# Expert tiles of two units of 128 slots with single units for the odd rest, in a fused deformable-convolution and expert kernel

## The chip, the core and the metric

The kernel runs on one core of a Trainium2 chip. The core has five engines with a queue of instructions each: PE (TensorE, matrix products), DVE (VectorE), ACT (ScalarE), POOL (GpSimd, which here only issues indirect DMAs) and SP (SyncE, which issues plain DMAs). Each engine works through its queue in order and waits on semaphores for the others; 16 DMA engines move the data. The metric is the device time in microseconds (us) of one execution of the whole program. Everything is computed in 32-bit floats.

## The reference

The input x has 4 images of 256 channels and 64 x 64 pixels. One layer is applied: three modulated deformable 3x3 convolutions with a residual, and then, on every pixel as a token of 256 values, a mixture of 8 experts with a residual. Cut to what matters here:

```python
x = x + conv3(ln_c(x))                    # three deformable convolutions with relu
t = to_tokens(x)                          # 4 x 4096 tokens of 256 values
z = ln_t(t)
probs = softmax(z @ gate_w + gate_b)      # 8 experts
top2_vals, top2_idx = top_k(probs, 2)
for e in range(8):                        # W1[e] is 256 x 512, W2[e] is 512 x 256
    y = gelu(z @ W1[e] + b1[e]) @ W2[e] + b2[e]
    out += cw[:, e] * y                   # cw: the top-two probability, else zero
t = t + out
```

The kernel computes each expert only for the tokens that chose it: each token takes two *slots*, one with each of its two experts.

## The kernel before, in words

**Convolutions.** An image is cut into 8 blocks of 512 pixels. A block of a layer takes nine *taps*; a tap makes four indirect gathers on POOL (L511, 128 rows of 4 KB, 0.52 MB each) of the four pixels around each sampling point, mixes them on DVE (L517, L522) and scales them on ACT (L525), turns them on PE (L540) and multiplies them with the tap's weights (L557). There are 4 x 3 x 8 = 96 blocks, 864 taps. Nine buffers hold gathered rows, so POOL can run about two taps ahead.

**Groups of tokens.** The tokens of images 0, 1 and 2 form three groups (0, 1, 2) of 4096 tokens, image 3 two groups (3, 4) of 2048. When the last block of a group is through, its lane `routes` runs `route` (L701): for each of the 128 x M tokens of a group (M is 32 or 16), from the ranks of its experts, the place of its two slots. Experts follow each other in a list of slots, and each expert's part is rounded up to whole tiles of FT = 256 slots, so that a tile has one expert. `NF` (L91) is the number of tiles that is always run, enough for the worst case: 2 x 32 x 128/256 + 7 = 39 in a large group, 23 in a small one, 163 in all. `invert` (L779) makes the list of tokens by slot (`tok`) with matmuls on one-hot matrices, and `wrow` holds for each tile the rows of the weight table that it needs.

**A tile.** `fetch` (L801) gathers the tile's weights on POOL (L811; 2308 floats on each of 128 partitions, 1.18 MB) and its tokens' rows (L823, one gather of 128 rows of 1 KB for each unit of 128 slots). The weight gather moves nothing where the tile before it in the list has the same expert (L764 to L766 set its rows out of bounds). Tiles are run in the order of `order` (L96): one from the first half of the list and one from the second in turn, each half with a weight buffer of its own (`w[step % 2]`). `expert` (L836) runs a tile in three pieces: four transposes of the rows (L851) and a copy to `zT` (L855); W1 as matmuls of 128x256 into `ph` (L867) and gelu (L877); W2 into `py` (L885). The trace counts 16 matmuls a tile at L867 and 16 at L885. The next tile is fetched between the second and the third piece, or ahead of the second while draining. `products` adds the bias on DVE (L903, which reads the weight buffer) and stores the tile to `ys` through SP (L906); it is called at the start of the next tile. When all tiles of a group are through, `combine_fetch` gathers each token's two results (L926), `combine` adds them weighted to the token (L941), and `give` turns and stores them.

**The order of the work.** Instructions are written out in one program order, and three lanes weave the expert work into the taps: after each tap `pump` gives every lane a credit of one tap, and a piece runs when its price is covered. A piece of a tile costs a third of the group's `pace`, in taps: 5, 6, 2, 1.5 and 0 for groups 0 to 4 (L983). At the end of some stages and of the program, `drain` runs pieces without taps, and group 4 is run wholly so. Each engine's queue keeps this order: a wait at one instruction holds all behind it.

## Time and profile before

| | |
|---|---|
| median of 3 runs | 6497.67 us (6488.08 to 6500.29) |
| the profiled execution | 6500.16 us |
| its span, first to last instruction | 6498.1 us |
| PE, DVE, POOL, ACT busy | 6025.0, 4960.6, 4424.2, 3330.6 us |
| moved by DMA | 2228.45 MB |

The span runs from the first to the last instruction of the profiled execution; about 2 us lie around it. In the groups of the profile, a line gives the source line, engine, operation, output and inputs, the shape and the count, then the busy time in us and the mean duration of one in ns, and then the time the engine stood idle just before these instructions with what ended it. In a table by stretch, each row gives the stretch in us from the span's start, its length, the busy time (and number of instructions) of PE, of PE's weight loads, of DVE, ACT and POOL, PE's granted clock, the mean busy share of the DMA engines, and GB/s. In a list of waits, each line gives who waited for whom, the total in us, how often, and the longest.

### The profile page before, as it was taken

The numbers are of one execution on the slowest core, as the hardware profiler recorded it, in microseconds if no ns is written. First come the engines' busy times: TensorE is split into PE (matmuls) and PEld (weight loads), VectorE is DVE, ScalarE is ACT, GpSimd is POOL, SyncE is SP. The second block draws the span as 40 slices with busy tenths as digits, with TensorE's granted clock in tenths as the row PEclk, the third lists the DMA queues.
The fourth block names the chain that finished last, engine by engine and source line by source line (L and its number), as shares of the span: only waits on it lengthen the run. The fifth ranks groups of instructions, "written<-read, shape, count | busy, mean of one in ns | idle before, by whom it ended". The sixth has DMA issues, their size and how long they took to land. (4 is left out here: it accounts for less than half of the span.)

```text
span 6498.1 us, 88881 instructions
## 1 busy us (share of the span) xinstructions
PE 6025.0 (93%) x26884; PEld 3542.5 (55%) x26884; DVE 4960.6 (76%) x11467; ACT 3330.6 (51%) x7139; POOL 4424.2 (68%) x4245
## 2 busy tenths in 40 slices
PE   7999998889999999999898999999988999988987
PEld 3444444444556555655454555555544666645765
DVE  7988888888977777888877877778888555687511
ACT  3555555555555555555454555555554444454322
POOL 4666776666767776666777777766777665677643
PEclk8999999999999999999999999999999999999998
DMA  8999999999999999999899999999999887898643
GB/s 279 388 368 382 408 403 409 372 365 355 356 354 393 365 368 380 358 360 358 316 354 352 399 372 374 373 368 371 385 375 337 297 294 264 295 357 316 229 143 123
DMA packets 805213, 2228.45 MB, mean 343 GB/s; under 512 B 105016, under 2 KB 307768, under 8 KB 798976
## 3 DMA queue, kind: packets, MB, share of 16 engines
q0 software_dynamic: 551200, 1947.35, 79.6%
q1 hardware_dynamic: 253536, 275.41, 12.3%
q8 instruction: 217, 3.56, 0.2%
q14 instruction: 260, 2.13, 0.1%
HBM read 2165.40 MB, written 196.40 MB: 363 GB/s over the span
## 5 line engine op out<-in xcount | busy, mean ns | idle before, releaser
L511 POOL DMA_INDIRECT g<-tab,idx x3456 | 3615.8, 1046 | 1516.8 <-issue 621.7
L557 PE MATMUL acc<-sT,wk 128*128 128x512 f32 x6912 | 3317.4, 601 | 13.5 <-ACT win L588 9.2
L517 DVE SCALAR_TENSOR_TENSOR g<-g,cf 128x512 f32<-128x512 f32 x3456 | 2559.5, 743 | 477.9 <-DMA g<-tab,idx 470.7
L525 ACT ACTIVATE s<-s,cf 128x256 f32<-128x256 f32 x3456 | 1669.2, 509 | 688.8 <-DVE s L522 638.2
L522 DVE SCALAR_TENSOR_TENSOR s<-g,cf 128x256 f32<-128x256 f32 x3456 | 1656.1, 482 | 466.2 <-PE tp L540 163.2
L557 PEld LDWEIGHTS acc<-sT,wk 128*128 128x128 f32 x6912 | 1193.0, 193 | 833.0 <-issue 800.1
L543 ACT COPY sT<-tp 128x512 f32<-128x512 f32 x1728 | 1010.7, 585 | 1238.8 <-PE tp L540 1230.9
L540 PEld LDWEIGHTS tp<-ident,s 128*128 128x128 f32 x6912 | 872.8, 144 | 1093.7 <-ACT s L525 543.8
L540 PE MATMUL tp<-ident,s 128*128 128x128 f32 x6912 | 1199.7, 280 | 204.6 <-ACT s L525 200.1
L867 PE MATMUL ph<-fzT,w 128*128 128x256 f32 x2608 | 651.2, 386 | 37.6 <-DMA w<-in_W,wrow 19.4
L885 PE MATMUL py<-w,hT 128*128 128x256 f32 x2608 | 639.7, 384 | 18.5 <-ACT hT L877 12.6
L867 PEld LDWEIGHTS ph<-fzT,w 128*128 128x128 f32 x2608 | 478.3, 192 | 164.2 <-ACT hT L877 36.4
L885 PEld LDWEIGHTS py<-w,hT 128*128 128x128 f32 x2608 | 477.8, 191 | 147.3 <-ACT hT L877 43.0
L877 ACT ACTIVATE hT<-ph,w 128x256 f32<-128x256 f32 x652 | 278.3, 470 | 477.4 <-PE ph L867 457.3
L823 POOL DMA_INDIRECT zt<-z,tok x326 | 336.7, 1033 | 161.6 <-issue 85.2
L811 POOL DMA_INDIRECT w<-in_W,wrow x163 | 177.8, 1091 | 261.7 <-issue 82.8
L926 POOL DMA_INDIRECT gy<-ys,slots x256 | 270.2, 1055 | 113.0 <-issue 71.0
L365 PE MATMUL po<-win,wo 128*32 128x504 f32 (+2 forms) x2560 | 306.8, 551 | 1.2 <-ACT win L588 0.6
L903 DVE TENSOR_TENSOR y<-py,w 128x512 f32<-128x512 f32 x163 | 111.5, 684 | 218.8 <-PE py L885 218.8
L941 DVE SCALAR_TENSOR_TENSOR ta<-gy,cw,ta 128x256 f32<-128x256 f32 x256 | 120.3, 478 | 100.0 <-DMA gy<-ys,slots 53.5
L365 PE MATMUL po<-win_pre,wo 128*32 128x504 f32 (+2 forms) x1280 | 173.9, 577 | 4.2 <-ACT om L374 3.5
L365 PEld LDWEIGHTS po<-win,wo 128*32 128x32 f32 x2560 | 70.9, 109 | 190.8 <-issue 150.6
(154 smaller groups left out, 2928.1 us busy)
## 6 DMA issues: line engine op xcount, KB each, us to landing
tab<-hv SPq DMA_DIRECT2D x512, 128.0 KB
g<-tab,idx POOLq DMA_INDIRECT x3456
ys<-y SPq DMA_DIRECT2D x163, 256.0 KB
tab<-h_pre SPq DMA_DIRECT2D x128, 256.0 KB
wk<-in_conv_w SPq DMA_DIRECT2D x117, 256.0 KB
xc_pre<-in_x SPq DMA_DIRECT2D x32, 512.0 KB
xr_tok<-in_x SPq DMA_DIRECT2D x32, 512.0 KB
t<-t_tok SPq DMA_DIRECT2D x32, 512.0 KB
```

What stands on the lines that cost most here:

```text
L365: nc.tensor.matmul(po[g * Q : (g + 1) * Q, :].rearrange("q (r w) -> q r w", w=W)[:, r0:r1, x0:x1], lhsT=self.wo[l][:, 3 * ky + kx, c, :], ...
L511: self.gathered = nc.gpsimd.indirect_dma_start(out=g.rearrange("p x s f -> p (x s f)"), out_offset=None, in_=self.table(*self.stages[i][:2 ...
L517: nc.vector.scalar_tensor_tensor(g[:, :, 0, :], g[:, :, 1, :], cf[:, j, 0:1], g[:, :, 0, :], ALU.mult, ALU.add,)
L522: self.last = nc.vector.scalar_tensor_tensor(s, g[:, 1, 0, :], cf[:, j, 1:2], g[:, 0, 0, :], ALU.mult, ALU.add)
L525: nc.scalar.activation(s, s, AF.Copy, scale=cf[:, j, 2:3])
L540: self.turned = nc.tensor.transpose(tp[:, c, u * P : (u + 1) * P], ss[u][:, c * P : (c + 1) * P], self.ident)
L543: nc.scalar.copy(self.sT[:, :, t0 * P : (t0 + 2) * P], tp)
L557: nc.tensor.matmul(self.acc[:, o, :], lhsT=self.wk[k][:, c, o * P : (o + 1) * P], rhs=sT[:, c, :], start=(k == 0 and c == 0), stop=(k == K ...
L823: self.nc.gpsimd.indirect_dma_start(out=zt, out_offset=None, in_=grp.zd, in_offset=bass.IndirectOffsetOnAxis(ap=grp.tok[:, j : j + 1], axi ...
L867: nc.tensor.matmul(ph[:, h, :], lhsT=w1[:, o : o + P], rhs=zT[:, c, :], start=(c == 0), stop=(c == CC - 1),)
L877: nc.scalar.activation(ht[:, h, :], ph[:, h, :], AF.Gelu, bias=w1[:, k : k + 1])
L885: nc.tensor.matmul(py[:, u, :], lhsT=hT[h // 2][:, h % 2, u * P : (u + 1) * P], rhs=w2[:, h * C : (h + 1) * C], start=(h == 0), stop=(h == ...
```

## The change

Slots are counted in units of 128 instead of tiles of 256. Each expert's part is rounded up to whole units (u of them); u // 2 pairs of units go to the front of the list, all experts' pairs in order, and the odd unit, where u is odd, goes behind all the pairs. The number of units that is always run is `NU` = 2 M + E - 1: 71 in a large group (78 before) and 39 in a small one (46 before). Of these the first 2 x `NP` (31 or 15 pairs) are run as tiles of two units, the nine others as tiles of one; where an input has more than `NP` pairs, the pairs left over are run as singles (`base` starts the odd units behind them). `NF` is the number of tiles, 40 or 24. A tile of one unit gathers one block of rows, makes its transposes and W1 products on 128 columns, and half the W2 products; its pieces cost half the pace. `route` works out both lists: counts, ends and offsets with a leading dimension of two, a comparison that tells which slots of an expert lie behind its pairs, and two comparisons instead of one for the expert of each tile.

```diff
-        self.NF = 2 * self.M * P // FT + E - 1
+        self.NU = 2 * self.M + E - 1
+        self.NP = (self.NU - E - 1) // FU
+        self.NF = self.NP + E + 1
...
+    def units(self, f):
+        return (FU * f, FU) if f < self.NP else (f + self.NP, 1)
...
-        nc.vector.tensor_scalar(ni, slot[:, :, M - 1], float(FT - 1), None, ALU.add)
-        nc.vector.tensor_scalar(ni, ni, FT_LOG, None, ALU.logical_shift_right)
-        nt = small("nt", (P, E))
-        nc.vector.tensor_copy(nt, ni)
-        end = small("end", (P, E))
-        nc.vector.tensor_tensor_scan(end, self.ones[:, :E], nt, 0.0, ALU.mult, ALU.add)
-        off = small("off", (P, E))
+        nc.vector.tensor_scalar(ni, slot[:, :, M - 1], float(P - 1), None, ALU.add)
+        two = small("two", (P, 2, E), I32)
+        nc.vector.tensor_scalar(two[:, 0], ni, FT_LOG, None, ALU.logical_shift_right)
+        nc.vector.tensor_scalar(
+            two[:, 1], ni, FT_LOG - 1, 1, ALU.logical_shift_right, ALU.bitwise_and
+        )
+        nt = small("nt", (P, 2, E))
+        nc.vector.tensor_copy(nt, two)
+        end = small("end", (P, 2, E))
+        for v in range(2):
+            nc.vector.tensor_tensor_scan(
+                end[:, v], self.ones[:, :E], nt[:, v], 0.0, ALU.mult, ALU.add
+            )
+        base = small("base", (P, 1))
+        nc.vector.tensor_scalar(
+            base, end[:, 0, E - 1 : E], float(FU), float(FU * grp.NP), ALU.mult, ALU.max
+        )
+        off = small("off", (P, 2, E))
         nc.vector.tensor_tensor(off, end, nt, ALU.subtract)
-        nc.vector.tensor_scalar(off, off, float(FT), None, ALU.mult)
+        nc.vector.tensor_scalar(off[:, 0], off[:, 0], float(FT), None, ALU.mult)
+        nc.vector.tensor_scalar(off[:, 1], off[:, 1], base, float(P), ALU.add, ALU.mult)
+        cut = small("cut", (P, E))
+        nc.vector.tensor_scalar(cut, nt[:, 0], float(FT), None, ALU.mult)
+        nc.vector.tensor_tensor(off[:, 1], off[:, 1], cut, ALU.subtract)
+        nc.vector.tensor_tensor(off[:, 1], off[:, 1], off[:, 0], ALU.subtract)
+        nc.vector.tensor_scalar(end[:, 0], end[:, 0], float(FU), None, ALU.mult)
+        nc.vector.tensor_scalar(end[:, 1], end[:, 1], base, None, ALU.add)
...
+        over = small("r1", (P, E, M))
+        nc.vector.tensor_tensor(over, slot, cut.unsqueeze(2).to_broadcast(every), ALU.is_ge)
         nc.vector.tensor_tensor(
-            slot, slot, off.unsqueeze(2).to_broadcast([P, E, M]), ALU.add
+            over, over, off[:, 1].unsqueeze(2).to_broadcast(every), ALU.mult
+        )
+        nc.vector.tensor_tensor(slot, slot, over, ALU.add)
+        nc.vector.tensor_tensor(
+            slot, slot, off[:, 0].unsqueeze(2).to_broadcast(every), ALU.add
         )
...
+        for v in range(2):
+            past = small("r1", (P, NF, E))
+            nc.vector.tensor_tensor(
+                past,
+                first.unsqueeze(2).to_broadcast([P, NF, E]),
+                end[:, v].unsqueeze(1).to_broadcast([P, NF, E]),
+                ALU.is_ge,
+            )
+            nc.vector.tensor_reduce(part if v else ex, past, AX.X, ALU.add)
+        nc.vector.scalar_tensor_tensor(ex, ex, float(E), ex, ALU.is_lt, ALU.mult)
+        nc.vector.tensor_tensor(ex, ex, part, ALU.add)
...
-        for u in range(FU):
+        q, fu = grp.units(f)
+        for u in range(fu):
             zt = self.ffn.tile([P, C], F32, tag=f"zt{u}", name=f"zt_{grp.nm}_{f}_{u}")
-            j = FU * f + u
+            j = q + u
...
-        nc.scalar.copy(zT, tp)
+        nc.scalar.copy(zT[:, :, :n], tp[:, :, :n])
...
-                        ph[:, h, :],
+                        ph[:, h, :n],
                         lhsT=w1[:, o : o + P],
-                        rhs=zT[:, c, :],
+                        rhs=zT[:, c, :n],
...
+                nc.scalar.activation(
+                    ht[:, h, :n], ph[:, h, :n], AF.Gelu, bias=w1[:, k : k + 1]
+                )
...
-        for u in range(FU):
+        for u in range(fu):
             for h in range(HC):
                 nc.tensor.matmul(
                     py[:, u, :],
...
-            self.ys[grp.i % 3][f * FT : (f + 1) * FT, :].rearrange("(u p) c -> p u c", u=FU),
-            y,
+            self.ys[grp.i % 3][q * P : (q + fu) * P, :].rearrange("(u p) c -> p u c", u=fu),
+            y[:, :fu],
...
+            pace = grp.pace * grp.units(grp.order[step])[1] / FU
             for _ in range(3 + (step == 0)):
-                self.tiles.put(grp.pace / 3, lambda gen=gen: next(gen, None))
+                self.tiles.put(pace / 3, lambda gen=gen: next(gen, None))
```

## The prediction

> **What bounds the kernel now.** I read the page's busy row and costliest groups first, then the engines by stretch (cut where the expert tiles of each group begin and end, found by the 163 copies fzT at L855), then the waits of single stretches and the PE timeline of the last one.
>
> The span (first line) and the groups and queue of the page that the change touches:
>
> ```profile
> PE 6025.0 (93%) x26884; PEld 3542.5 (55%) x26884; DVE 4960.6 (76%) x11467; ACT 3330.6 (51%) x7139; POOL 4424.2 (68%) x4245
> ...
> q0 software_dynamic: 551200, 1947.35, 79.6%
> ...
> L867 PE MATMUL ph<-fzT,w 128*128 128x256 f32 x2608 | 651.2, 386 | 37.6 <-DMA w<-in_W,wrow 19.4
> L885 PE MATMUL py<-w,hT 128*128 128x256 f32 x2608 | 639.7, 384 | 18.5 <-ACT hT L877 12.6
> ...
> L811 POOL DMA_INDIRECT w<-in_W,wrow x163 | 177.8, 1091 | 261.7 <-issue 82.8
> ```
>
> PE leads with 93%, but an average hides stages. By stretch (columns: stretch, PE, PE loads, DVE, ACT, POOL, clock, DMA share, GB/s): a convolution without experts, then groups 0, 1, 2, 3 and 4:
>
> ```profile
> 650.00:1000.00 350.00, 330.97 (x1375) 164.08 (x1374) 309.11 (x596) 206.94 (x443) 255.54 (x256) 1.00 1.02 406
> 1756.00:3066.00 1310.00, 1289.86 (x5843) 769.21 (x5842) 1052.46 (x2380) 727.03 (x1583) 915.92 (x884) 0.99 0.98 369
> 3251.00:4755.00 1504.00, 1446.59 (x6323) 842.29 (x6322) 1195.46 (x2449) 827.86 (x1789) 1111.11 (x1075) 0.99 0.98 372
> 5034.00:5708.00 674.00, 644.26 (x2881) 428.94 (x2878) 392.55 (x787) 318.44 (x676) 425.05 (x419) 0.99 0.82 287
> 5934.00:6230.00 296.00, 278.26 (x1259) 209.53 (x1257) 145.27 (x392) 110.78 (x234) 169.78 (x166) 0.96 0.66 225
> 6230.00:6445.00 215.00, 191.19 (x862) 153.52 (x860) 29.74 (x56) 54.05 (x125) 88.51 (x92) 0.98 0.44 139
> ```
>
> With groups 0 and 1, PE (96 to 98%) and DMA (0.98) are both full: a gain on PE soon meets DMA. With groups 2 to 4, DMA falls to 0.82, 0.66, 0.44 and PE bounds alone. Waits while group 2 runs:
>
> ```profile
> DVE g L517 <- DMA g<-tab,idx: 216.4, 114, 9.4
> ...
> POOL w L811 <- ACT s L525: 55.8, 17, 5.1
> POOL w L811 <- ACT hT L877: 25.4, 8, 4.1
> ```
>
> DVE waits for gathers that a DMA at 0.82 could serve: POOL, in order, stands at a weight fetch until its buffer is free, and the gathers stand behind it. PE in the last group (start, duration, line):
>
> ```profile
> 6197.65 2.86 PE L885 MATMUL py<-w,hT 128*128 128x256 f32 x12 [0.19 <-ACT hT L877]
> 6200.35 1.89 PE L867 MATMUL ph<-fzT,w 128*128 128x256 f32 x8
> 6202.07 0.60 PE L959 MATMUL otp<-ident,ta 128*128 128x128 f32 x4
> ```
>
> Tiles repeat every 8.2 us there (copies at 6197.85, 6206.05, 6214.25), with next to no PE idle time.
>
> [...]eight 128x256 matmuls take 1.73 us (0.216 each) though each load lasts 0.19, and four 128x128 transposes take 0.60 with the last one's 0.27 in it, so 0.11 each. [...]after a weight wait, eight L867 matmuls took 3.66 us at 6273.1. [...] The chain of waits has 5.8, 6.8 and 7.2; I use those.
>
> **The change part by part.** 326 units run before (163 tiles of two), 3 x 71 + 2 x 39 = 291 after: 35 fewer, 7 in each of the five groups, in 168 tiles (123 pairs, 45 singles).
>
> PE. A pair costs 4 transposes 0.43, 16 ph 3.46, 16 py 3.45: 7.34 us, 3.67 a unit. A single halves py and the transposes by count and ph by width. Unknown: 128-column ph matmuls at 0.11 us (half) or at the load's 0.19 us (then 16 x 0.08 = 1.3 us more, 45 singles: 58 us). The 16 lp_tok matmuls of 8 columns take 1.81 us, 0.113 each with the same 0.19 us loads; I take half. Saved: 35 x 3.67 = 128 us, 25.7 a group.
>
> DMA. Each lost unit saves a zt gather and a ys store, 131 KB each: 35 x 0.262 = 9.2 MB. Weights are fetched only where a tile's expert differs from its neighbour's. Counting the reference's routing of its own inputs: nine fetches a group before, 45 in all. The page confirms this: gathers 3456 x 0.524 = 1812, zt 43, gy 34, 45 x 1.182 = 53, rest 6: 1947 MB in q0. Singles bring experts in anew: 13, 12, 12, 13, 12 fetches, 62 in all: +20.1 MB. Net +10.9 MB, of which +4.6 MB in groups 0 and 1 (12 us at 372 GB/s).
>
> POOL loses 35 zt issues and gains 5 w issues: 30 x 1.05 = 32 us on an engine with 68%; nothing, except through w's waits below. SP stores are five more and smaller; ACT's gelus narrower: hidden behind PE.
>
> Route adds DVE work per group: six ops of 8 values (about 0.2), five more small ones, three of 256 values (0.41 as L736), one more compare and reduce (0.47 + 0.46): about 4.5 us, 3.6 in half groups; 21 in all. DVE is 80% busy in groups 0 and 1 and behind it stand the sample sums. I charge half, 4 us for those two and 3 for the last group, whose route lies among draining tiles; uncovered it is 21.
>
> Lane pace: a single has half the taps, so a group's tiles end 17.5 taps (group 0), 21 (group 1), 7 (group 2) earlier and those taps run without experts. Their speed decides the exposure.
>
> Groups 0, 1. Group 1 moves 372 x 1504 = 559 MB, 31 of it for experts (39 x 0.524 + 9 x 1.18). Without these and at the share of 1.02 seen without experts (387 GB/s), 1365 us: the 39 tiles cost 139 us, 3.6 each, half of 7.34. Group 0 likewise: 452 MB at 384, 1177 of 1310, 3.4. So half of 2 x 25.7: 26. Less half the added DMA (6) and route (4): **16**.
>
> Group 2. 38 tile steps in 674 us with 273 gathers, 68 taps. Without experts at 7.2 us a tap (the 226 us after it hold 125 gathers) they cost 4.8 a tile, 66%; at 5.5 (256 gathers in the first stretch) 100%. I take 0.8: 20.6. The new cost: POOL may issue a fetch only when the y add two tiles back has read the buffer, and a tile is now one tap instead of two, so the gathers' lead over PE shrinks; 3 more fetches x 2 us, and 5 for the lead: **10**. Bounds: 0 and 30 us of stall.
>
> Group 3, half woven, half draining: 25.7 x 0.7 = 18, less 4 fetches x 2: **10**.
>
> Group 4 drains. Before: 203.4 us from first to last copy, 22 x 8.2 = 180 of it, 23 of weight waits (11 at the start, 1.7, 4.0, 1.3, 3.7, 0.9 later). After: 15 x 8.2 against a single's 3.67 plus gelu latency 1.2 = 4.9, x 9: 167 in place of 23 x 8.2 = 189, saves 21.5. Fetch steps 1, 4, 5, 11, 13, 15, 17 follow pairs (1.5 each as now), 8, 12, 16, 20 follow singles: 6 us of landing against 4.9 + 2.5 - 4.2 = 3.2 of cover, 3 each. Waits 33.5, 10.5 more: 11, less route and odds: **9**.
>
> Sum 16 + 10 + 10 + 9 = 45. The profiled execution took 6500.16 (span 6498.1 and 2.1 around it), 2.5 above the median and at the top of the runs: 6500 - 45 = **6455**.
>
> **Rivals.** *All of it shows*: DMA has slices at 409 GB/s, so PE alone decides: 6500 - 128 + 15 for routes and fetches, below 6415, about 6390. Against: DMA's 0.98 in 2814 us.
> *Hidden*: groups 0 and 1 are bound by bytes, lose 12 and 5 for route, groups 2 to 4 keep half of 29: about 6500 + 17 - 15, 6485 to 6511.
> *Slower*: the fetch wait on POOL. Now L811 idles 261.7 us before 163 issues, 1.6 each. Singles sit at every second step of the latter half of a group, so about 90 steps have half the distance; if each waits 1.6 us twice more and two thirds reach PE: 90 x 3.2 x 0.67 = 193, against a gross gain of 26 + 21 + 18 + 21 = 86 less the 13 for bytes and routes: up to 6620; above 6511 from 1.4 us a step on (84). For it: the waits above. Against: at paces of 5 and 6 taps L811 hardly waits; only groups 2 to 4 are short.
> That fewer units do not run is excluded: the loop's length is fixed at 71.
>
> **How the numbers follow.** Forecast (6415 to 6485) 0.57, all of it 0.13, hidden 0.15, slower 0.15. Against the median, 0.2% (13 us) is about what a measurement can tell from no change; below 6485 is faster: 0.70, same 0.15, slower 0.15. The range 6405 to 6515 leaves some 0.1 at each end: its low end is most of the 128 us, its high end the stalls; the forecast's own range is 6415 to 6485.
>
> **What would show it.** L867 in two widths, the 128-column one near 0.11 us a piece in a run (at 0.19, PE's gain is half). PE busy some 110 to 150 us lower. q0 up by 20 - 4.6 = 15 MB. The stretch of group 0 shorter by about 17.5 taps (119 us at 6.8), that of group 1 by 21 (138 at 6.56), and the freed taps after them near 5.5 to 6.3 us each; group 4 about 10 us shorter. Wrong if L811's waits or PE's wait for w grow beyond 40 us, if DMA's share in groups 0 and 1 reaches 1.0 with PE idle, or if DVE's route burst opens a PE gap.

## The result

The changed kernel takes 6483.85 us (median of 12 runs, 6479.17 to 6493.5) where the kernel before takes 6499.41 beside it: a ratio of 0.9979, with a 95% interval of 0.9972 to 0.9987. The change is a gain, but of 14 us (by the ratio) to 16 us (by the medians) in place of the 45 forecast. As the experiments below show, some 6 to 7 of these have nothing to do with the size of the tiles. The median lies 1 us inside the forecast's range of 6415 to 6485.

The first lines are the busy row and the gather queue from the page of the changed kernel (profiled span 6484.0 us); then its groups of instructions with each shape apart (busy, mean ns of one, idle before with what ended it):

```profile
PE 5947.8 (92%) x26614; PEld 3470.3 (54%) x26614; DVE 4968.3 (77%) x11562; ACT 3298.5 (51%) x7156; POOL 4421.0 (68%) x4215
...
q0 software_dynamic: 550240, 1962.85, 79.9%
```

```profile
L928 PE MATMUL py<-w,hT 128*128 128x256 f32 x2328 | 581.5, 386 | 26.7 <-ACT hT L918 17.9 <-DVE y L947 5.6 <-ACT o L1012 1.0
L908 PE MATMUL ph<-fzT,w 128*128 128x256 f32 x1968 | 502.1, 392 | 43.4 <-DMA w<-in_W,wrow 33.4 <-ACT fzT L896 9.3 <-ACT hT L918 0.7
...
L849 POOL DMA_INDIRECT w<-in_W,wrow x168 | 181.0, 1077 | 319.4 <-ACT hT L918 79.7 <-issue 67.5 <-ACT s L529 54.2
L908 PE MATMUL ph<-fzT,w 128*128 128x128 f32 x720 | 99.8, 281 | 4.2 <-ACT fzT L896 2.3 <-ACT hT L918 1.2 <-DMA w<-in_W,wrow 0.3
```

The change does what it says: 1968 + 720 matmuls of W1 in two widths, 2328 of W2 (8 a unit, 291 units), 15.5 MB more in q0. PE's work at ph, py and the transposes fell from 1394 us to 1278 (transposes 103.5 to 94.7), by 116. Little of it reached the span, which is 14 us shorter: PE's other work grew by 39 us (its busy time as a whole fell by 77) and its idle time by 63, from 473 to 536. PE waits longer for weights (33.7 us over both widths, 19.4 before), and POOL stands 319.4 us ahead of its weight gathers, 261.7 before.

The engines by stretch, for the stretches that answer to those of the kernel before (no experts, then the tiles of groups 0 to 4):

```profile
650.00:1000.00 350.00, 333.31 (x1392) 166.53 (x1391) 312.11 (x604) 208.22 (x448) 255.09 (x260) 1.00 1.03 413
1751.00:2954.00 1203.00, 1181.44 (x5325) 703.08 (x5326) 946.34 (x2088) 660.06 (x1454) 841.24 (x809) 0.99 0.96 367
3271.00:4644.00 1373.00, 1327.99 (x5902) 775.46 (x5900) 1089.16 (x2201) 754.21 (x1655) 1010.14 (x977) 0.99 0.99 376
5057.00:5659.00 602.00, 582.19 (x2692) 392.00 (x2691) 354.38 (x695) 284.51 (x636) 374.94 (x371) 1.00 0.84 296
5932.00:6225.00 293.00, 262.84 (x1207) 194.29 (x1207) 142.92 (x403) 108.64 (x239) 156.79 (x154) 0.94 0.67 230
6225.00:6432.00 207.00, 171.49 (x798) 135.56 (x798) 29.04 (x57) 49.95 (x129) 83.26 (x86) 0.94 0.47 154
```

The tiles of groups 0, 1 and 2 end 107, 131 and 72 us sooner after they begin (119 and 138 were forecast for the first two); the taps freed by that run without experts and take it back. In the last two groups the clock is 0.94, where it was 0.96 and 0.98. The waits while group 2 runs:

```profile
DVE g L521 <- DMA g<-tab,idx: 153.7, 103, 6.3
...
POOL w L849 <- ACT s L529: 35.4, 13, 5.1
POOL w L849 <- issue: 29.6, 11, 5.7
POOL w L849 <- ACT sT L547: 23.7, 7, 7.0
```

And PE in the last group, a single and the pair behind it:

```profile
6298.93 1.05 PE L908 MATMUL ph<-fzT,w 128*128 128x128 f32 x8
...
6307.94 3.39 PE L908 MATMUL ph<-fzT,w 128*128 128x256 f32 x8 [3.72 <-DMA w<-in_W,wrow]
6311.90 0.70 PE L928 MATMUL py<-w,hT 128*128 128x256 f32 x2 [0.56 <-ACT hT L918]
6312.44 1.89 PE L908 MATMUL ph<-fzT,w 128*128 128x256 f32 x8
```

Eight W1 matmuls of a single take 1.05 us, half a pair's 1.89: the unknown of the prediction came out as taken. The pair behind waits 3.72 us for its weights, and its first eight matmuls then take 3.39, at a granted clock of 0.58 (1.00 in the second eight, which take 1.89).

**Where the time went.** Both traces have the same 96 convolution blocks, and the copy out of `acc` (L588 before, L592 after) ends each. The table cuts the profiled executions where these copies begin and gives the difference to the kernel before in us. The first 18 tiles of group 2 run in blocks 83 to 86; they are pairs in every kernel, and the lane that combines group 1 ends there, so the cut behind block 86 puts the singles of group 2 into the next column. One profiled execution scatters: the padded kernel before, which differs from the kernel before by three small stores, stands at +6, -8 and -5 in the last three columns, so differences under 8 us in these are not read. The three profiles of the tiling before (as it is, padded, shifted) have a mean of +4, -4 and -3 there, the three of the changed tiling +2, +2 and -9. The runs are described in the next part.

| kernel | blocks 0 to 6 | 7 to 16 | 17 to 26 | 27 to 86 (groups 0, 1) | 87 to 92 (group 2) | 93 to end (groups 3, 4) |
|---|---|---|---|---|---|---|
| before, us | 519.9 | 499.9 | 603.7 | 3749.2 | 479.0 | 646.5 |
| predicted | 0 | 0 | 0 | -16 | -10 | -19 |
| changed | -1.5 | -7.1 | -2.5 | +5.6 | +0.5 | -9.0 |
| changed, padded | +0.5 | -6.5 | -0.6 | +3.0 | +6.3 | -7.2 |
| changed, shifted | -0.6 | -0.2 | +1.1 | -4.0 | -1.2 | -10.7 |
| route only | -0.1 | -0.4 | -0.6 | +17.4 | -5.7 | -0.3 |
| two tiles less | +0.5 | -6.5 | +0.1 | -23.1 | -8.6 | -42.0 |
| no odd weights | +3.1 | -6.2 | -2.1 | -7.5 | -1.9 | -10.9 |
| no late weights | +0.2 | -6.9 | -2.1 | -1.3 | -7.1 | -48.7 |
| no late fetch | +0.4 | -7.1 | -2.1 | -19.2 | +5.4 | -57.6 |
| combined | -1.0 | -6.9 | -1.7 | -31.7 | +2.7 | -23.7 |
| singles in 3, 4 only | -1.1 | -0.2 | -1.1 | +13.1 | -4.4 | -4.5 |
| full pace | -1.6 | -5.5 | -1.8 | -19.9 | +2.5 | +7.2 |
| odd tiles at the end | -8.7 | -6.7 | -2.2 | +28.0 | -1.0 | -18.9 |
| before, no late weights | -0.1 | -0.1 | +0.6 | +5.2 | -7.1 | -8.6 |
| before, padded | +1.0 | -0.2 | -0.2 | +6.2 | -8.0 | -5.4 |
| before, shifted | +2.7 | -7.0 | +0.9 | +6.4 | -3.6 | -2.8 |

Groups 0 and 1 gained nothing that can be told, group 2 nothing, groups 3 and 4 some 6 to 9 us, and 7 us came from blocks 7 to 16, ahead of any expert tile.

### The profile page after: what moved, and what is told of

It reads as the page before. It is cut to its first block, busy times and chain, and to the rows that moved or that the text cites. A ratio compares the mean times of both kernels' runs of the same rounds, so it can differ in the third digit from the quotient of the medians.

```text
span 6484.0 us, 88406 instructions
## 1 busy us (share of the span) xinstructions
PE 5947.8 (92%) x26614; PEld 3470.3 (54%) x26614; DVE 4968.3 (77%) x11562; ACT 3298.5 (51%) x7156; POOL 4421.0 (68%) x4215
## 5 line engine op out<-in xcount | busy, mean ns | idle before, releaser
L561 PE MATMUL acc<-sT,wk 128*128 128x512 f32 x6912 | 3340.8, 604 | 14.0 <-ACT win L592 8.7
L561 PEld LDWEIGHTS acc<-sT,wk 128*128 128x128 f32 x6912 | 1199.5, 194 | 830.9 <-issue 799.1
L908 PE MATMUL ph<-fzT,w 128*128 128x256 f32 (+1 forms) x2688 | 601.9, 363 | 47.6 <-DMA w<-in_W,wrow 33.7
L928 PE MATMUL py<-w,hT 128*128 128x256 f32 x2328 | 581.5, 386 | 26.7 <-ACT hT L918 17.9
L908 PEld LDWEIGHTS ph<-fzT,w 128*128 128x128 f32 x2688 | 459.9, 195 | 165.5 <-issue 35.7
L918 ACT ACTIVATE hT<-ph,w 128x256 f32<-128x256 f32 (+1 forms) x672 | 267.7, 442 | 501.4 <-PE ph L908 486.1
L928 PEld LDWEIGHTS py<-w,hT 128*128 128x128 f32 x2328 | 423.4, 191 | 147.4 <-ACT hT L918 54.4
L862 POOL DMA_INDIRECT zt<-z,tok x291 | 296.0, 1017 | 158.7 <-issue 74.5
L849 POOL DMA_INDIRECT w<-in_W,wrow x168 | 181.0, 1077 | 319.4 <-ACT hT L918 79.7
L947 DVE TENSOR_TENSOR y<-py,w 128x512 f32<-128x512 f32 (+1 forms) x168 | 103.2, 614 | 246.6 <-PE py L928 243.9
```

The lines of the kernel that those rows point to most:

```text
L561: nc.tensor.matmul(self.acc[:, o, :], lhsT=self.wk[k][:, c, o * P : (o + 1) * P], rhs=sT[:, c, :], start=(k == 0 and c == 0), stop=(k == K ...
L862: self.nc.gpsimd.indirect_dma_start(out=zt, out_offset=None, in_=grp.zd, in_offset=bass.IndirectOffsetOnAxis(ap=grp.tok[:, j : j + 1], axi ...
L908: nc.tensor.matmul(ph[:, h, :n], lhsT=w1[:, o : o + P], rhs=zT[:, c, :n], start=(c == 0), stop=(c == CC - 1),)
L928: nc.tensor.matmul(py[:, u, :], lhsT=hT[h // 2][:, h % 2, u * P : (u + 1) * P], rhs=w2[:, h * C : (h + 1) * C], start=(h == 0), stop=(h == ...
```

## The experiments

Medians in us, each with that of the kernel before on the same chip, and the ratio with its 95% interval:

| run | kernel | time | before | ratio |
|---|---|---|---|---|
| e1 | route only | 6518.28 | 6500.17 | 1.0032 (1.0020 to 1.0044) |
| e2 | singles in groups 3, 4 only | 6507.94 | 6500.17 | 1.0015 (1.0008 to 1.0023) |
| e3 | no odd weights | 6472.7 | 6500.17 | 0.9962 (0.9950 to 0.9974) |
| e4 | before, two tiles less a group | 6422.81 | 6500.17 | 0.9881 (0.9866 to 0.9896) |
| e5 | no late weights | 6432.83 | 6500.33 | 0.9897 (0.9882 to 0.9912) |
| e6 | full pace | 6480.74 | 6500.33 | 0.9975 (0.9963 to 0.9986) |
| e7 | no late fetch | 6414.14 | 6500.33 | 0.9867 (0.9852 to 0.9883) |
| e8 | odd tiles at the end | 6486.68 | 6500.33 | 0.9977 (0.9969 to 0.9985) |
| e13 | combined | 6452.67 | 6500.03 | 0.9931 (0.9914 to 0.9947) |
| e14 | before, no late weights | 6488.62 | 6500.03 | 0.9973 (0.9958 to 0.9987) |
| e15 | changed, padded | 6484.33 | 6500.03 | 0.9975 (0.9967 to 0.9983) |
| e16 | before, padded | 6503.6 | 6500.03 | 1.0003 (0.9994 to 1.0012) |
| e17 | before, shifted | 6494.57 | 6496.81 | 0.9992 (0.9984 to 0.9999) |
| e18 | changed, shifted | 6491.2 | 6496.81 | 0.9988 (0.9982 to 0.9995) |

### Part by part: the route, the units

**Route only (e1).** The new route with pairs alone, 39 and 23 tiles as before: the edit sets NP to the number of tiles and the count of odd units to zero.

```diff
+        if not single:
+            self.NF = self.NP = self.M * P * 2 // FT + E - 1
+            self.NU = FU * self.NF
...
+            nc.vector.memset(two[:, 1], 0)
```

> The new route, but with no odd units in any group: 39 or 23 tiles of two units as before the change, 45 weight fetches. The output is the full one. It isolates the longer route. Theory A (the route's added DVE work of about 5 us a group reaches the path, as the block in which group 0 is routed was 5 us longer in the trace of after): 10 to 18 us slower than the kernel before. Theory B (the route is hidden behind PE and DMA): within 4 us of before.

Measured: 18 us more than the kernel before by the medians, 21 by the ratio. Block 27 holds the route of group 0. The stretch of block 27, of the kernel before and then of this one:

```profile
1623.50:1680.40 56.90, 55.45 (x266) 31.11 (x267) 55.38 (x156) 29.51 (x63) 44.02 (x35) 1.00 0.89 322
```

```profile
1622.40:1684.40 62.00, 56.45 (x271) 31.78 (x269) 59.14 (x175) 31.05 (x64) 44.10 (x37) 0.97 0.87 317
```

DVE, third in the row, is busy 55.38 of 56.90 us before and 59.14 of 62.00 after: 19 more instructions (156 to 175), 3.8 us, and the block is 5.1 longer; PE, first in the row, stands idle 5.55 us in place of 1.45. DVE at 80% over the whole of groups 0 and 1 hid a burst in which it is busy 97% of the time. Blocks 81 and 82, with the route of group 2, are 10.1 us longer together; blocks 50 to 52, with that of group 1, are not. So in sum the route shows about in full, but not in every group. It doesn't stand alone in this run either: 50 of its gathers bring weights, one more in each group than before (q0 1953.26 MB), where 45 had been expected, and what these five cost was not tried.

**Singles in the last two groups only (e2).** As e1, with single units in groups 3 and 4.

```diff
+        odd = (3, 4)
+        self.groups = [Group(b, 0, NB, b in odd) for b in range(last)]
...
```

> Single units only in groups 3 and 4 (image 3), pairs only in groups 0 to 2, with the new route everywhere. The output is the full one. If the singles of groups 0 to 2 were worth nothing, as the trace of after says (no gain at the end of the last convolution block, all of it in the drain behind it), this run equals the changed kernel within 6 us. If they were a gain of 20 us or more hidden by something else, it is 20 us slower than the changed kernel; if they are a loss, faster than it by that loss.

Measured: 10 us below e1. The singles of groups 3 and 4 gain 10, where the prediction had 10 and some 11 ahead of the route. The rest of the step to the changed kernel, 23 us, is the singles of the large groups with the 6 to 7 us that are shown further down not to be theirs: some 16 us for them, about what the route costs.

**Two tiles less (e4).** The kernel before with 37 and 21 tiles; two tiles of each group's worst case are left out, 20 units in all.

```diff
-        self.NF = 2 * self.M * P // FT + E - 1
+        self.NF = 2 * self.M * P // FT + E - 3
```

> The kernel before with two tiles fewer in each group, 37 and 21: 20 units less in all, no singles, no added fetch, the old route. This input fills at most 37 and 20 tiles, so the output is the full one. It prices a unit that simply goes. At my forecast's prices (half of 3.67 us in groups 0 and 1, 0.8 and 0.7 in 2 and 3, all in 4) 20 units are 55 us: 45 to 60 us faster than before if the units are worth what I put down and the singles' own costs ate it. If units in the woven stages are worth little whatever their form: 15 to 25 us faster, nearly all of it in the drain.

Measured: 77 us less, where 45 to 60 had been expected. Taking off the 6.5 of blocks 7 to 16, 71 us for 20 units: 3.5 a unit against the 3.67 of its PE work. In groups 0 and 1, 23.1 for 8 units is 2.9 each (a scatter of 6 us makes it 2.1 to 3.6), in place of the 1.7 to 1.8 (3.4 and 3.6 a tile) of the prediction. In groups 3 and 4 it is 42.0 for 8 units, 5.3 each, more than their PE work; a part of that may be the two gathers that bring weights fewer (43). If 35 units were worth as much as these 20, they would bring some 123 us (an estimate from this run), and something takes over 110 of them.

### What takes it: weights behind a single

**No odd weights (e3).** The singles' gathers bring no weights (they multiply with what lies in the buffer: their weights are left out of the computation). The gathers stay as instructions; 41 of them move data, 62 in the changed kernel.

```diff
+        nc.vector.memset(same[:, grp.NP :], 1.0)
```

> The changed kernel, but single units fetch no weights and use those in the buffer, so the weights of the odd units are not the right ones: 47 or so fetches in place of 62, 18 to 20 MB less. Theory W (the added weight bytes and the waits for them ate the gain on PE): 20 to 40 us faster than the changed kernel. Theory P (a single costs PE and the queues nearly as much as its share of a pair plus a fixed part, weights hardly matter while taps run): at most 10 us faster, and that in the drain.

Measured: 11 to 12 us below the changed kernel, between what its two theories had. Their weights, 24.8 MB of q0 (1938.04 here), would take 67 us at 372 GB/s; the kernel gains 12 without them, all of it in groups 0 and 1 by the table (13 us), where nine of the 21 gathers lie (10.6 MB, 29 us at that rate). So bytes cost about half their time in groups 0 and 1, where the DMA engines are full (share 0.96 and 0.99 in the changed kernel), and nothing that can be told elsewhere. PE's waits for weights stay as they were (34.1 us here, 33.7 in the changed kernel): they do not come from the singles' own gathers.

**No late weights (e5).** As e3, and the pairs that run between singles bring none either (27 gathers move data; these pairs' weights are left out too).

```diff
+        nc.vector.memset(same[:, grp.NP :], 1.0)
+        nc.vector.memset(same[:, grp.NP - grp.half + 1 : grp.half], 1.0)
```

> As the run without weights for the single units, and besides no weights for the pairs that run between singles (steps 24 on in a large group, 8 on in a small one): 27 fetches in all, 14 fewer than in that run; those tiles use what is in the buffer, so their weights are not the right ones. The instructions stay and move nothing. Theory C (a single has half a pair's length, so the next pair's fetch, which before hid behind a whole pair, is waited for): 25 to 45 us faster than the run without single weights, that is 50 to 70 us faster than before. Theory P (each single costs PE time beyond half a pair, whatever is fetched): 5 to 12 us faster than that run, the share of the bytes alone.

Measured: 40 us below e3, and the table puts 38 of them into groups 3 and 4. W1 of the pairs, and the stretch from block 95 to the end, of e3:

```profile
L909 PE MATMUL ph<-fzT,w 128*128 128x256 f32 x1968 | 504.4, 394 | 44.5 <-DMA w<-in_W,wrow 34.1 <-ACT fzT L897 9.7 <-ACT hT L919 0.7
```

```profile
6081.88:6472.70 390.82, 291.25 (x1368) 227.83 (x1366) 90.17 (x269) 87.16 (x215) 160.78 (x165) 0.87 0.42 128
```

and of e5:

```profile
L910 PE MATMUL ph<-fzT,w 128*128 128x256 f32 x1968 | 491.4, 386 | 21.1 <-DMA w<-in_W,wrow 11.1 <-ACT fzT L898 9.3 <-ACT hT L920 0.7
```

```profile
6077.95:6432.20 354.25, 277.55 (x1368) 219.36 (x1366) 90.26 (x270) 87.16 (x215) 160.97 (x165) 0.90 0.39 118
```

PE's waits for weights fall from 34.1 to 11.1 us (23, nearly all in this stretch), and PE's busy time in the stretch falls by 13.7 for the same 1368 matmuls (12.0 of it at W1 of the pairs), with the clock at 0.90 in place of 0.87. Together some 36, as much as the stretch is shorter (36.6). In sum these waits are paid about one and a half times: once as idle time, and again by half in slower matmuls. It is not so for each: of the changed kernel's 13 waits, the four under 1 us have no slow matmuls behind them, and of the nine from 2.49 us up seven do (eight W1 matmuls in 2.90 to 3.75 us in place of 1.89, at a granted clock of 0.50 to 0.66) and two, of 2.88 and 3.19, do not (1.99, at 1.00).

**No late fetch (e7).** As e5, with the gathers of these steps left out as instructions (83 in place of 168).

```diff
+        if not (f >= grp.NP or grp.NP - grp.half < f < grp.half):
+            self.nc.gpsimd.indirect_dma_start(
+                out=self.w[step % 2][:, : W1N + W2N],
...
```

> As the run without late weights, but the weight instructions of those steps are left out altogether, so POOL doesn't stand at them until a buffer is free (their weights are not the right ones either). Theory H (POOL, held at L811's place by the buffer of two steps before, keeps the gathers behind it waiting): 15 us or more faster than the run without late weights. If that wait is harmless: within 6 us of it (the issue times of 1.05 us on POOL go).

Measured: 19 us below e5, though the gathers taken away moved nothing. By the program POOL, in order, stands at each until the weight buffer has been read; the lists of waits show how long, not that this is the reason. The waits of POOL at weight gathers in blocks 42 to 48 (group 0 with singles in the changed kernel), in the kernel before,

```profile
POOL w L811 <- issue: 2.7, 9, 0.3
...
POOL w L811 <- ACT s L525: 0.6, 2, 0.3
```

and in the changed kernel:

```profile
POOL w L849 <- DVE g L521: 14.2, 2, 10.5
DVE g L521 <- DMA g<-tab,idx: 13.9, 25, 1.6
...
POOL w L849 <- ACT s L529: 9.6, 2, 9.3
...
POOL w L849 <- issue: 7.4, 8, 5.0
POOL w L849 <- PE tp L544: 7.2, 2, 6.9
```

Waits of up to 10.5 us, 38 us in sum where there were under 4. These seven blocks hold 24 units in the kernel before and 25 in the changed kernel, e5 and e7. They are 21.4 us longer in the changed kernel, 21.3 in e5 and 3.1 in e7: 18 of the 21 come with the gather instructions, and none with their bytes. The seven blocks of e5 and of e7:

```profile
2508.70:2974.42 465.72, 450.58 (x2084) 274.80 (x2083) 389.21 (x1000) 262.19 (x573) 310.90 (x294) 0.97 0.93 344
```

```profile
2506.78:2954.36 447.58, 436.35 (x2078) 270.02 (x2077) 381.97 (x1008) 265.68 (x575) 300.37 (x277) 0.99 0.97 359
```

Most of the 18 us (14.2) is PE's busy time, for nearly the same matmuls at a clock of 0.99 in place of 0.97. The way from POOL to PE is argued, not shown: DVE, which never waited for gathers in these blocks before, waits 13.9 us for them in the changed kernel, but still 20.4 in e7, so the sum of its waits does not measure the loss. And e7 takes away, with the wait, the issue of 16 gathers here (1.0 us each on POOL, which is busy two thirds of the time); the kernel before issues 13 in these blocks without loss, so the wait is the likelier cause, but no run parts the two.

**The control (e14).** The kernel before with the weights of the same span of steps left out: all its tiles are pairs.

```diff
+        g0 = 12 if M == 32 else 4
+        nc.vector.memset(same[:, g0 : grp.half], 1.0)
+        nc.vector.memset(same[:, grp.half + g0 - 1 :], 1.0)
```

> A control on the kernel before: its weight gathers move nothing for the steps of the latter part of each group, the same span of steps that brought no weights in the kernel without late weights (tiles 12 and on of the first half of a large group's list and 11 and on of the second; 4 and 3 in a small group); those tiles multiply with the weights that lie in the buffer, which is left out of the computation. Theory C (a pair's fetch is late because the tile ahead of it is a single, half as long as a pair): in the kernel before every tile is a pair, so taking the fetches away gains only the five short waits of the last group and the bytes, 10 to 18 us together: 6482 to 6490. Rival (the fetches of that part are late whatever lies ahead of them): 35 us or more, 6465 or below, as the changed kernel gained 42 from the same step.

> As for the first run of this kernel, beside a kernel before of about 6500 us. Theory C (the pairs' fetches are late because a half-length single is ahead of them): 6482 to 6490, a gain of 10 to 18 us. Rival (fetches of that part are late whatever is ahead of them): 6465 or below, 35 us or more.

Measured: 11 us below the kernel before (the first text was written for a chip spoken of below); 26 gathers bring weights, 45 in the kernel before. Its W1, with 10.4 us of waits for weights, 19.4 in the kernel before:

```profile
L870 PE MATMUL ph<-fzT,w 128*128 128x256 f32 x2608 | 649.6, 385 | 26.1 <-DMA w<-in_W,wrow 10.4 <-ACT fzT L858 9.0 <-ACT hT L880 6.2
```

The same span of steps without weights gains 52 us in the changed kernel (e5 to changed, by medians beside their own kernel before), 12 of them from the singles' own gathers (e3). Groups 3 and 4 compare best: ten gathers fewer gain 8.6 us by the table where all tiles are pairs, and from e3 to e5 eight fewer gain 38 where singles stand between the pairs. So about 30 are due to the tile ahead being a single, as the theory has it, and not to late fetches as such.

### Pace and order

**Full pace (e6).** A single costs the lanes a whole pace, as a pair.

```diff
-            pace = grp.pace * grp.units(grp.order[step])[1] / FU
+            pace = grp.pace
```

> The changed kernel with a single's pieces at the full pace of a pair: 40 tiles at 5, 6, 2 and 1.5 taps, so the same work and bytes as the changed kernel, a large group's tiles spread over as many taps as before the change and one tile more, and twice the time between a single's pieces. The output is the full one. Theory C: 10 to 25 us faster than the changed kernel (waits for weights in groups 0 to 3 go, the drain of group 4 stays). Theory P: within 8 us of the changed kernel.

Measured: 4 us below the changed kernel, no difference that counts, where the theory had 10 to 25. POOL's longest wait at a weight gather in group 0's blocks 42 to 48 is 0.3 us again. These blocks are 32.8 us shorter than in the changed kernel, but with 18 units in place of 25, so that most of it is tile work put off. Up to block 92 the run is some 21 ahead; from 93 to the end it loses 16, which is why the theory's gain does not show in the whole.

**Odd tiles at the end (e8).** All pairs first, in the two halves of their own list, then the nine singles; a pair then has a pair ahead of it. 64 gathers move weights.

```diff
+        self.order = [s // 2 + s % 2 * self.half for s in range(self.NP)]
+        self.order += range(self.NP, self.NF)
...
```

> The changed kernel in another order: the pairs first, one from each half in turn, then the nine singles one after the other on both weight buffers in turn, with the weights fetched wherever the buffer holds another expert (and none for tiles that hold no slot): 64 fetches. The output is the full one. Theory C: pairs' fetches are covered by pairs again, the singles' are not: 10 to 20 us faster than the changed kernel, 25 to 35 faster than before. Theory P: within 6 us of the changed kernel.

Measured: as the changed kernel in sum, where the theory had 10 to 20 us less. From 93 to the end -18.9 in place of -9.0, but +28.0 in groups 0 and 1. Why the order costs so much there was not tried.

**Combined (e13).** Full pace in groups 0 to 2, odd tiles at the end in groups 3 and 4 (there with half pace).

```diff
+        self.groups += [Group(last, 0, NB // 2, True), Group(last, NB // 2, NB, True)]
...
+            pace = grp.pace
+            if grp.at_end:
+                pace *= grp.units(grp.order[step])[1] / FU
```

> The changed kernel with two edits taken from runs: in groups 0 to 2 a single costs the lanes as much as a pair (as in the kernel at full pace, which stood 26 us ahead of the kernel before at block 92 but lost 10 in the draining part), and in groups 3 and 4 the pairs run first and the nine singles last (as in the kernel with the odd tiles at the end, which gained 23 us between block 95 and the end). If the two parts don't meddle with each other: 26 + 19 to 23 = 45 to 49 us faster than the kernel before, 6451 to 6455. If the gain at block 92 is only work put off into the draining part: 6475 to 6482, no better than either alone.

> As for the first run of this kernel, now beside a kernel before of about 6500 us: 6451 to 6455 if the two parts add up (26 us ahead of the kernel before at block 92, and 19 to 23 more from block 95 to the end); 6475 to 6482 if the gain at block 92 is only work put off into the draining part.

Measured: 6452.67, 47 us below the kernel before and 31 below the changed kernel, as expected if the parts add up, from four executions (6437.47 to 6463.88). This beats both kernels. Its profiled execution took 15 us less than its median (span 6435.7), so that its row in the table is somewhat too good; but -23.7 from 93 on and -31.7 in groups 0 and 1 are where they were looked for. PE's waits for weights are still 29.3 us, nearly half of it (13.3) now at the singles.

### The 7 us ahead of the experts

Blocks 7 to 16 hold no expert work, yet they were 5.5 to 7.1 us shorter in every kernel with fewer units and as before in e1 and e2. The first guess was where the DRAM tensors lie, since `ys` is smaller.

**Padded kernels (e15, e16).** Three DRAM tensors of seven units behind the three of `ys`, in the changed kernel and in the kernel before.

```diff
+            self.pads.append(
+                self.dram.tile([7 * P, C], F32, name=f"pad_{i}", tag=f"pad_{i}")
+            )
```

> The changed kernel with a DRAM tensor of seven units (7 x 128 rows) placed behind each of the three smaller ys tensors, so that every tensor behind them lies as far off as in the kernel before. Nothing else changes but three stores of 4 KB at the start. Theory D (some 7 to 9 us of the measured gain come from where the DRAM tensors lie, since blocks 7 to 26, which run no expert work and are the same program, were 7 to 9 us shorter in all kernels with a smaller ys): those blocks take as long as in the kernel before, within 2 us, and the whole is 6490 to 6494, 7 to 9 us slower than the changed kernel and 6 to 9 faster than the kernel before. Rival (that stretch varies for a reason that has nothing to do with the size of ys[...]): the padded kernel is as the changed one, 6484, within 3 us.

> As for the first run of this kernel, beside a kernel before of about 6500 us and a changed kernel of 6484. Theory D (placement of the DRAM tensors): blocks 7 to 26 as long as in the kernel before, within 2 us, and the whole 6490 to 6494. Rival: blocks 7 to 26 as in the changed kernel, 6484 within 3 us.

> The kernel before with the same three DRAM tensors of seven units behind its ys tensors, and so with another placement of all that follows; no other change but three stores of 4 KB at the start. Theory D: blocks 7 to 26 change by some us, most likely 5 to 9 shorter as with every other size of ys that was run, so 6491 to 6495; a placement that happens to be as good as the old one would show no change and would leave the theory to the run with the padded changed kernel. Rival: 6500, within 3 us, with blocks 7 to 26 as before.

> As for the first run of this kernel, beside a kernel before of about 6500 us. Theory D: blocks 7 to 26 change, most likely 5 to 9 us shorter, 6491 to 6495. Rival: 6500 within 3 us, blocks 7 to 26 as before.

Measured: 6484.33 and 6503.6, blocks 7 to 16 at -6.5 and -0.2. The theory falls: padding does not change these blocks. What sets the kernels with the gain apart is elsewhere: the change resizes the lists `tok` and `wrow` and the route's small tiles, and the nine SBUF buffers of gathered rows lie behind them. They begin at byte 192256 of a partition (a multiple of 256) in the changed kernel and at 191744 (a multiple too) in e4, but at 191808 in the kernel before and 192352 in e1 and e2, 64 and 96 bytes past one.

**Shifted kernels (e17, e18).** A tile of 192 bytes a partition more in the kernel before (buffers at 192000, a multiple), of 64 in the changed kernel (192320, 64 past one).

```diff
+        shift = self.rt.tile([P, 48], F32, tag="shift", name="shift")
+        nc.vector.memset(shift, 0.0)
```

> The kernel before with a tile of 192 bytes a partition more ahead of the buffers of gathered rows, so that these begin at 192000, a multiple of 256, in place of 191808, 64 past one. Theory S (where the gathered rows land in SBUF): blocks 7 to 16 are 6 to 8 us shorter and the whole 6491 to 6494. Rival (anything else that the change brings): 6500 within 3 us, blocks 7 to 16 as before.

> The changed kernel with a tile of 64 bytes a partition more ahead of the buffers of gathered rows, so that these begin at 192320, 64 past a multiple of 256 as in the kernel before, in place of 192256, a multiple. Theory S: blocks 7 to 16 as long as in the kernel before, and the whole 6490 to 6494, 6 to 9 us slower than the changed kernel. Rival: 6484 within 3 us, blocks 7 to 16 as in the changed kernel.

Measured: blocks 7 to 16 at -7.0 and -0.2. The effect changes sides with the address alone. One stretch in these blocks (GB/s last, instructions of POOL in brackets before the clock), of the kernel before,

```profile
665.00:1015.00 350.00, 328.83 (x1367) 162.93 (x1366) 307.50 (x592) 205.37 (x440) 255.63 (x256) 1.00 1.03 406
```

the kernel before shifted,

```profile
665.00:1015.00 350.00, 331.29 (x1385) 165.75 (x1384) 311.45 (x601) 207.80 (x446) 256.68 (x260) 1.00 1.03 413
```

the changed kernel,

```profile
665.00:1015.00 350.00, 330.35 (x1383) 164.85 (x1385) 310.31 (x600) 208.38 (x448) 254.62 (x259) 1.00 1.03 413
```

and the changed kernel shifted:

```profile
665.00:1015.00 350.00, 328.99 (x1368) 163.14 (x1367) 307.48 (x592) 206.43 (x440) 255.17 (x256) 1.00 1.03 406
```

406 GB/s with the buffers off a multiple of 256 bytes, 413 on one, at the same DMA share. The shift also moves other small buffers, which DVE, ACT and PE use. But in this stretch the gathers' packets of 4096 bytes take 160.3 ns on average in the changed kernel and 162.8 in the kernel before, while one sum of samples on DVE (743 ns), one scaling on ACT (508 and 509) and one convolution matmul (593) take as long in both. So it is the transfers that change. Of the whole, the kernel before gains only 2 us by the medians (5 by the ratio, interval 0.6 to 10), less than the 6 to 9 expected; where the rest goes, one profile does not show. The changed kernel shifted is at 0.9988 against 0.9979, 6 us worse. With the buffers as the kernel before has them, the tiling itself gains 8 us (0.9988, interval 3 to 12), and with both on a multiple about as much (0.9979 against 0.9992).

### Another chip

The first runs of four of these kernels (e9 to e12, whose expectations stand above) were made on a chip on which the kernel before takes 7419.23 us. Beside it the padded changed kernel took 7459.27 (1.0066, 1.0042 to 1.0091), the padded kernel before 7412.94 (1.0011), the kernel before without late weights 7416.46 (1.0002), the combined one 7420.0 (1.0002, 0.9988 to 1.0016). The DMA lines of the padded kernel before and of the combined one there:

```profile
DMA packets 805645, 2228.46 MB, mean 301 GB/s; under 512 B 105448, under 2 KB 308200, under 8 KB 799408
```

```profile
DMA packets 799851, 2239.32 MB, mean 302 GB/s; under 512 B 103080, under 2 KB 301352, under 8 KB 791440
```

Where the other chips move 343 GB/s over the span, this one moves 301, even the 47 us of the combined kernel are gone, and the changed tiling, padded, is 0.7% slower. That would be so if the experts' work were hidden there, as in the *Hidden* rival of the prediction, but no run tests it. Whether bytes, latency or the lower clock (0.92 to 0.93 over the span, 0.97 elsewhere) is the cause was not tried.

## Why the prediction was wrong

The direction was right, the size a third. Three steps failed: the waits of POOL and PE for weights behind a single, put at nothing in groups 0 and 1 (e7: 19 us) and at their landing time alone in groups 3 and 4 (e5: 38 us); the route at half its DVE work (e1: 18 to 21 us, where 7 were charged); and, the other way, a unit's worth in groups 0 and 1 at half its PE time. That the errors left a gain at all, just inside the range, is partly luck: 7 of the 14 us come from an address that the prediction knows nothing of. By its own steps:

- **PE.** Right. The 128-column matmuls run at half (1.05 us for eight, 1.89 at 256 columns). The three PE groups fell by 116 us where 128 were forecast; W1 of the pairs takes 392 ns each in place of 386, some 12 us in all, and is back at 386 in e5, without the late weights. PE as a whole fell by only 77: the 6912 convolution matmuls (L557, then L561) took 23 us more, and the mean clock over the span fell from 0.976 to 0.968.
- **DMA bytes.** Right in size: 15.5 MB more in q0. In groups 0 and 1 half their time was charged (6 of 12 us), and half is about what e3 shows for the singles' weights there (13 of 29).
- **A unit's worth in groups 0 and 1.** Too small: half its PE time was taken, 1.7 to 1.8 us, and e4 measured 2.9. The working split the stretch by its bytes, since the DMA share was 0.98; but PE was at 96 to 98%, and its share of the price came out larger.
- **Route.** 7 us charged ("I charge half"; 4 for groups 0 and 1, 3 for the last, none for 2 and 3), 18 to 21 measured, five more weight gathers in it. The DVE work itself was sized right (4.5 us forecast, 3.8 in block 27). The average of DVE over a stage was read for a burst of some 60 us in which DVE is at 97%. The PE gap that the prediction named as a sign of being wrong is there (5.55 us in place of 1.45 in block 27).
- **"POOL loses 35 zt issues and gains 5 w issues ... nothing, except through w's waits".** The exception was the matter. Only group 2 was given a stall, "5 for the lead"; groups 0 and 1 got none ("L811 hardly waits"). But a single at half pace stands 2.5 or 3 taps behind its neighbour, POOL is held at the weight gather for up to 10.5 us, and the sample gathers stand behind it: e7 gives 19 us for these instructions, 18 of them in seven blocks of group 0. L811's waits grew by 58 us, beyond the 40 that the prediction named as a sign of being wrong.
- **Group 2.** -10 forecast, +0.5 measured (+6.3 and -1.2 in the two other profiles of this tiling): no gain that can be told. DVE's waits for gathers did not grow (216.4 us in 674, then 153.7 in 602); which of this step's terms failed, the runs do not separate.
- **Groups 3 and 4.** -19 forecast, -9.0 measured (-7.2, -10.7; 6 against the mean of the three profiles of the tiling before). The single's step was right (4.9 forecast; in the trace a pair and a single take 12.8 to 13.0 together, a pair alone 8.2). The late fetches "3 each" behind singles (from a landing of 6 us; the weight gathers in the chain of the kernel before take 5.83 to 7.24) were about right as waits (0.3 to 5.6 us). What was left out is the clock behind most of the long ones: after waits of 3.72 and 5.57 us eight W1 matmuls took 3.39 and 3.75 in place of 1.89, at a granted clock of 0.58 and 0.50. The prediction had one such case of the kernel before, 3.66 us for eight matmuls at 6273.1 (3.64 in the trace, at a clock of 0.53, after a wait of 2.12), and did not charge it for the new waits. e5 puts waits and clock together at 38 us in these two groups. In group 4's sum, 11 less the 3 named for the route is 8, not 9.
- **What had no term at all**: 7 us in blocks 7 to 16, from an SBUF address.

So 45 became 14: the 14 units of groups 0 and 1 were worth 40 (14 x 2.9) and not 26, but route (17 in e1) and weight gathers (25 between the changed kernel and e7, bytes and waits) took all of it; the 14 of groups 3 and 4 gave 6 to 9 in place of 19; group 2 nothing in place of 10; and the address gave 7. Each of these figures is from single profiles and good to some 6 us.

Of the rivals, *Hidden* (6485 to 6511) misses the time by 1 us, and has not the mechanism, as units are worth nearly their full price in e4. *Slower* has the mechanism: the weight gather as a wait on POOL and, from there, on PE. It was forecast at up to 193 us; e5 and e7 together show 59, of which the pairs-only control has 11 too. *All of it shows* is the time that e7 reaches: 6414, with the late weights and the waits for them left out.

## What to carry to other kernels

When a loop's steps are made shorter, first list what was fetched one step ahead: it now has half the cover, a miss is paid as idle time and, if it is long, again in slow matmuls (here 23 us and 14), and what stands behind it in the same queue waits too (19 us in e7, by the likelier reading). Give the short steps the pace of the long ones where other work is woven in, and put them last where there is none: here the two together turned 16 us into 47, though neither did alone, and on another chip nothing came of it. And judge an added burst on an engine by the stretch in which it falls, not by the stage's average.

## What the runs showed of the hardware

The address of a gather's target in SBUF counts: in the stretch from 665 to 1015 us, in blocks 7 to 16, where the DMA engines are full (share 1.03), the core moves 413 GB/s with the buffers of gathered rows at a multiple of 256 bytes (192256 in the changed kernel, 192000 in the kernel before shifted) and 406 with them 64 past one (191808 in the kernel before, 192320 in the changed kernel shifted): 1.7%. A packet of 4 KB takes 160.3 ns in the changed kernel and 162.8 in the kernel before, 1.5%. e1, 96 past a multiple (192352), moves 406 too. Multiples of 512 (192000) and odd multiples of 256 (192256, and 191744 in e4) have blocks 7 to 16 shorter by 7.0, 7.1 and 6.5 us. Why the address counts is not shown, and the runs do not tell 256 from 128.
